# Twenty-five norms' rows transposed by DMA in two-byte halves instead of on TensorE

## The chip, the core and the metric

The kernel runs on one core of a Trainium2 chip, in one launch. The core has a matrix engine (TensorE, in the profile PE, with its weight loads as PEld), VectorE (DVE), ScalarE (ACT), GpSimd (POOL) and SyncE (SP), which here only issues DMAs. Each engine runs its own instructions in program order; they wait for one another by semaphores. Matmul results land in PSUM, everything else lies in SBUF. The metric is the device time of one execution in microseconds, the median of several runs.

## The reference

Eight batches of 512 rows with 256 features, fp32, go through four steps, each a normalisation of the rows and a residual addition:

```python
x = x + attn_a(layernorm(x), W_q, W_k, W_v)      # linear attention: q, k to unit length,
                                                 # q * sum over rows of (k * v) / 512
x = x + ffn(layernorm(x), W_r, W_k, W_v, mu_r, mu_k)
x = x + attn_b(layernorm(x), q_w, q_b, k_w, k_b, v_w, v_b, l_w, l_b)  # 16 heads of 64
x = x + ffn(layernorm(x), W_r, W_k, W_v, mu_r, mu_k)

def ffn(x):                                      # x_prev: the row before, zero for the first
    xr = mu_r * x + (1 - mu_r) * x_prev
    xk = mu_k * x + (1 - mu_k) * x_prev
    return sigmoid(xr @ W_r.T) * (relu(xk @ W_k.T) ** 2 @ W_v.T)

def attn_b(x):                                   # softmax over the queries (axis 2)
    scores = (x q_w + q_b) (x k_w + k_b).T / 8
    return concat(softmax(scores, axis=2) @ (x v_w + v_b)) @ l_w.T + l_b
```

There are therefore 4 x 8 = 32 layernorms. After each one a matmul over the features follows, so the normalised rows are needed with the features on the partitions: they have to be transposed.

## The kernel before, in words

Work goes in halves of a batch: h is 0 or 1, a half has 256 rows, two tiles of 128 rows by 256 features. The names a, f, n and g stand for the norms before the linear attention, the first feed-forward part, the softmax attention and the second feed-forward part; a tile's name ends in batch or half number.

`normed_t` (from L348) makes one half of a norm: VectorE takes mean and variance (L354, L355), GpSimd raises the variance to the power -0.5 (L373 to L375), ScalarE writes the normalised rows `xn` (L378), and TensorE turns them in four 128x128 transposes into one PSUM bank `tr_...` (L386). What reads that bank depends on the norm. For a (`linear`, L513) and n (`front`, L593) ScalarE copies it into SBUF (L519 into `xp`, L612 into `xta`). In `ffn` (L414, for f and g) ScalarE scales it twice straight from PSUM (L429), VectorE mixes PSUM and the scaled, shifted rows into `xk` and `xr` (L443), and only then is the bank given back.

The softmax attention runs in pairs of heads. `scores` (L907) multiplies keys and queries into a PSUM pair (L919), VectorE takes the maxima (L924), `exps` (L929) lets ScalarE exponentiate and sum (L935), GpSimd divides v by the sums (`scale_v`, L952), and `context` (L959) multiplies (L972). `attend` (L985) writes these in a fixed order for two pairs of heads.

All other work is put between these stretches by a planner that runs while the program is built. Every chain of steps (`linear`, `queries`, `front`, `ffn`, `project_pairs`, `values_fast`, `project_out`) is a Python generator that yields, before each step, the engine (T, A, V, G), the step's cost in microseconds and the time its input is ready. `Order` keeps a clock for each engine and picks the step to write next, with due dates in periods (one period for each two pairs of heads). `fill` writes whatever is ready beside the current TensorE time, `until` what is due, `CHOICES` holds for each period three numbers that vary its share of work, its slack and the order of equals. Since every engine runs in the order written, the order is fixed before the kernel starts. The costs decide the order; the waits at run time are semaphores.

[...] three pairs of banks that scores take turns on, and two single ones for the contexts; products and transposes borrow free ones. SBUF buffers `xn`, `xp`, `xr`, `xk` exist in two sets, "False" and "True"; `r` shares memory with `xk`, and `ka` with `xn`. The set "True" serves batch 1's front and, later, the g norms of batches 0 to 6.

SyncE issues the weights and inputs at the start, later each half's output (L876) and, when both halves of a batch are out, the load of the batch four further on (L264).

Of the kernel before, what the change touches and what calls it, by code (L numbers as in the profile page):

```python
# [7 lines left out]

F32 = mybir.dt.float32
AF = mybir.ActivationFunctionType  # L10
ALU = mybir.AluOpType
AX = mybir.AxisListType

P = 128
B, S, D = 8, 512, 256
# [13 lines left out]
CHANGE = 0.1  # L29
PAIRS, BANKS = 3, 2  # L30
X_LANDS = (4.1, 8.5, 12.0)
PASS = {"T": 0.27, "A": 0.2, "V": 0.17, "G": 0.17}

CHOICES = (
    (-2, 1, 55171), (-6, 2, 40869), (0, 0, 0), (-2, 1, 0), (0, -1, 58232), (6, 0, 85741),
    (6, -1, 2853), (0, 0, 0), (-6, -1, 27454), (0, -1, 74092), (0, 0, 2161), (2, 1, 0), (6, 0, 0),
    (-6, 0, 93887), (0, 0, 0), (4, 2, 61401), (0, 0, 0), (1, 1, 45112), (-2, 0, 99964),  # L40
    (-1, 0, 87739), (0, 0, 37516), (6, -1, 75545), (2, -1, 48345), (-1, 0, 55064), (0, -1, 12544),
    (-4, 0, 88217), (0, 0, 0), (4, 2, 76141), (1, 0, 10517), (4, -1, 38996), (6, 1, 66702),
    (-4, 0, 67700), (0, 0, 0), (0, 0, 0),
)


# [27 lines left out]
class Order:  # L74
# [3 lines left out]


    def __init__(self):  # L80
        self.free = {"T": 0.0, "A": 0.0, "V": 0.0, "G": 0.0}
        self.chains, self.period, self.spent, self.count = [], -1, 0.0, 0
        self.marks = {None: 0.0}

        self.banks = [0.0] * (PAIRS + BANKS)
        self.current, self.at = None, 0.0
# [103 lines left out]
    def fill(self, budget=0.0, slack=1.0):  # L190


        begin = self.spent
        late = {"V": slack, "A": slack, "G": slack + 2.0}
        while True:
            a = [
                c for c in self.able(2 * (budget - (self.spent - begin)))
                if (self.start(c) <= self.now + 0.2 if c.on == "T"
                    else self.start(c) + c.cost <= self.now + late[c.on])
            ]  # L200
            if not a:
                return
            self.run(self.first(a))
# [24 lines left out]
def kernel(ctx: ExitStack, tc: tile.TileContext, a: dict, out: bass.AP):  # L228
# [116 lines left out]

        return t[:, h, :].rearrange("p (t d) -> p t d", t=2)

    def normed_t(src, name, s, h, ready, mark=None, early=False):  # L348

        ready = yield "V", 1.2, ready  # L350
        mv = small.tile([P, 2, 2], F32, tag="mv", name=f"mv_{name}_{h}")
        for u in range(2):
            st = small.tile([P, 6], F32, tag="st", name=f"st_{name}_{h}_{u}")
            nc.vector.bn_stats(st, src[:, 2 * h + u, :])  # L354
            nc.vector.bn_aggr(mv[:, u, :], st)  # L355
        xn, rstd = inner(s["xn"], h), small.tile([P, 2], F32, tag="rstd", name=f"rstd_{name}_{h}")
        if early:

            ready = yield "G", 1.05, ready
            nc.gpsimd.tensor_scalar(rstd, mv[:, :, 1], LN_EPS, 1.0, ALU.add, ALU.mult)  # L360
            nc.gpsimd.tensor_tensor(rstd, rstd, neg_half[:, :2], ALU.pow)
            ready = yield "V", 0.75, ready
            for u in range(2):
                nc.vector.tensor_scalar(
                    xn[:, u, :], src[:, 2 * h + u, :], mv[:, u, 0:1], rstd[:, u : u + 1],
                    ALU.subtract, ALU.mult,
                )
        else:

            shift = small.tile([P, 2], F32, tag="shift", name=f"shift_{name}_{h}")  # L370
            nc.vector.tensor_scalar(shift, mv[:, :, 0], -1.0, None, ALU.mult)
            ready = yield "G", 1.3, ready
            nc.gpsimd.tensor_scalar(rstd, mv[:, :, 1], LN_EPS, 1.0, ALU.add, ALU.mult)  # L373
            nc.gpsimd.tensor_tensor(rstd, rstd, neg_half[:, :2], ALU.pow)
            nc.gpsimd.tensor_tensor(shift, shift, rstd, ALU.mult)  # L375
            ready = yield "A", 1.0, ready
            for u in range(2):
                nc.scalar.activation(  # L378
                    xn[:, u, :], src[:, 2 * h + u, :], AF.Identity,
                    bias=shift[:, u : u + 1], scale=rstd[:, u : u + 1],  # L380
                )
        ready = yield "T", 0.55, ready, -1, mark
        ps = bank(f"tr_{name}_{h}").rearrange("p (k s) -> p k s", k=KC)
        for kc in range(KC):
            for u in range(2):
                nc.tensor.transpose(  # L386
                    ps[:, kc, u * P : (u + 1) * P], xn[:, u, kc * P : (kc + 1) * P], ident
                )
        return ps, ready

    def rows(name, lhs, rhs):

# [18 lines left out]

    edge = {}

    def ffn(xb, name, s, h, ready, add_on):  # L414


        ps, ready = yield from normed_t(xb, name, s, h, ready)

        parts = ((1, s["xn"]), (0, s["xp"]))
        if not edge:  # L420
# [19 lines left out]
        for (i, y), dst in zip(parts, (xk, xr)):  # L440
# [5 lines left out]
                )  # L446
            if i == 1:
                mixed = ready
        order.give()
        done = yield "T", BANK, mixed  # L450
        ps = bank(f"k_{name}_{h}")
        for dc in range(KC):
# [49 lines left out]
    def adder(b):  # L502

        return nc.vector if b < 2 else nc.gpsimd
# [8 lines left out]
    def linear(b, h):  # L513

        xb, s = x[b], buffers(b == 1)
        ps, ready = yield from normed_t(xb, f"a{b}", s, h, asked[b] + X_LANDS[min(b, 2)] + h / 2, early=b < 2)
        xt, kv = inner(s["xp"], h), inner(s["ka"], h)
        ready = yield "A", 0.5, ready
        nc.scalar.copy(xt, ps)  # L519
        order.give()  # L520
        order.marks[f"a{b}", h] = ready
        ss = small.tile([P, 2], F32, tag="ss", name=f"ssk_{b}_{h}")
        arrived = ready
        for u in range(2):
            ready = yield "T", BANK, arrived
            ps = bank(f"kv_{b}_{h}_{u}")
            for kc in range(KC):
                nc.tensor.matmul(  # L528
                    ps, lhsT=xt[:, kc, u * P : (u + 1) * P], rhs=wkv[:, kc, :],
                    start=(kc == 0), stop=(kc == KC - 1),  # L530
                )
            ready = yield "A", 0.8, ready
            vs = two.tile([P, D], F32, tag="av", name=f"av_{b}_{h}_{u}")
            nc.scalar.copy(vs, ps[:, D:])
            sq = one.tile([P, D], F32, tag="sq", name=f"sqk_{b}_{h}_{u}")
            nc.scalar.activation(sq, ps[:, :D], AF.Square, accum_out=ss[:, u : u + 1])
            if u == 1:
                order.add(queries(b, h), *due_of(b))
            ready = yield "V", 0.35, ready
            nc.vector.tensor_mul(kv[:, u, :], ps[:, :D], vs)  # L540
            order.give()
        rn = small.tile([P, 2], F32, tag="rn", name=f"rnk_{b}_{h}")
        ready = yield from power(rn, ss, b, h, 0, ready)

        for u in range(2):
            ready = yield "V", 0.39, ready
            if b not in means:
                means[b] = kv[:, u, :]
                nc.vector.tensor_scalar(means[b], kv[:, u, :], rn[:, u : u + 1], None, ALU.mult)
            else:  # L550
                nc.vector.scalar_tensor_tensor(
                    means[b], kv[:, u, :], rn[:, u : u + 1], means[b], ALU.mult, ALU.add
                )
        if both(f"a{b}"):
            order.add(mean(b, ready), *due_of(b))
# [37 lines left out]
    def front(b, h, gf, ready):  # L593
# [7 lines left out]
                qs[:, u, :], qs[:, u, :], rn[:, u : u + 1], gf, ALU.mult, ALU.mult  # L601
            )
        ready = yield from add_to(xb, h, s["r"][:, h, :], ready, adder(b))
        ready = yield from ffn(xb, f"f{b}", s, h, ready, adder(b))


        last = f"qk_{NP * (b - 1) - 2}" if b > 1 else None
        ps, ready = yield from normed_t(xb, f"n{b}", s, h, ready, last)
        ready = yield "A", 0.5, ready
        if b not in xta:  # L610
            xta[b] = two.tile([P, KC, S], F32, tag="xta", name=f"xta_{b}")
        nc.scalar.copy(xta[b][:, :, h * HS : (h + 1) * HS], ps)  # L612
        order.give()
        order.marks[f"n{b}", h] = ready
        if not both(f"f{b}"):
            if b == 0:
# [251 lines left out]
    def tail(b, h, ready):  # L868

        last = b == B - 1  # L870

        add_on = nc.vector if last else nc.gpsimd
        yield from ffn(x[b], f"g{b}", buffers(not last), h, ready, add_on)
        ts = slice(2 * h, 2 * h + 2)
        rows_out = out[b].rearrange("(t p) d -> p t d", p=P)
        nc.sync.dma_start(out=rows_out[:, ts, :], in_=x[b][:, ts, :])  # L876
        if both(f"g{b}") and b + 4 < B:
            load_x(b + 4)
            add_front(b + 4)
# [105 lines left out]
    def attend(g):  # L985

        for c in range(NT):
# [5 lines left out]
            else:  # L993
                order.fill(BANK)
            exps(g, c)
            order.fill()
        for c in range(NT):
            scores(g + 1, c)
            if c == 1:
# [3 lines left out]
            if c == 3:  # L1003
                context(g, 3)
            exps(g + 1, c)
            order.fill()


    G = B * NP
# [23 lines left out]


    total = B * (2.2 + 6 * BANK + 42 * FAST + 0.43 + 8 * BANK + 2 * FFN) - 4 * BANK - 2 * FFN
    total += 2 * FAST
    for first in range(0, G, 2):
        g = order.period = first + 1
# [73 lines left out]
```

## Time and profile before

| What | us |
|---|---|
| median of three runs (1163.23 to 1165.66) | 1163.61 |
| the profiled execution, its own time | 1162.87 |
| its span, first to last instruction | 1161.0 |
| ScalarE: exps L935, 512 instructions | 346.6 busy |
| VectorE: maxima L924, 256 instructions | 309.2 busy |
| TensorE: scores L919, contexts L972 | 262.9 and 260.3 busy |
| TensorE: transposes L386, the four groups of 56 for a, f, n and g | 9.5, 8.5, 8.3 and 8.2 busy, 273 to 299 ns each |
| GpSimd: scaling of v L952, 128 instructions | 78.7 busy |

The profile is of one execution, so sums are made against its own time. The granted TensorE clock was 0.999 of full speed. A duration in the tables is that of one instruction; matmuls overlap one another in the pipeline, so their durations add up to more than the time that they take, and the distance between the starts of neighbours says what one of them costs. "Idle before" a group is time in which its engine stood still just before the group's instructions, with the instruction that ended the wait. An engine's idle time costs nothing as long as TensorE has work.

### The profile page before, as it was taken

To read this page: it belongs to the slowest core of one execution; us is meant where nothing else is said; L and a number is where in the kernel's file an instruction comes from. 1 tells how busy PE (TensorE), PEld (TensorE's weight loads), DVE (VectorE), ACT (ScalarE), POOL (GpSimd) and SP (SyncE) were. 2 spreads that over 40 slices of the span, in tenths; PEclk is the share of its full clock that TensorE was granted. 3 is DMA by queue.
4 is the path that set the end of the run, shared out by engine and by line. 5 is a ranking of instruction groups with operands and counts; after the bars stand their busy time and mean duration, and the time that the engine had idled before them with its cause. 6 is when DMAs were issued, how large, how long until landed. Compare 5 with 4: busy or idle time off the path is not lost.

```text
span 1161.0 us, 19258 instructions
## 1 busy us (share of the span) xinstructions
PE 1143.5 (98%) x7212; PEld 719.5 (62%) x7212; DVE 772.9 (67%) x1384; ACT 679.3 (59%) x1776; POOL 422.7 (36%) x602
## 2 busy tenths in 40 slices
PE   6999999999999999999999999999999999999998
PEld 3655466655667566666666666766557666666657
DVE  5677675766667677575777674757757666657754
ACT  4557664766545756456655574755764565654743
POOL 5374243523335233443333433323344223332311
PEclk9999999999999999999999999999999999999999
DMA  8000000000000000000000000000000000000001
GB/s 294 1 1 2 1 1 1 2 1 10 28 1 1 2 1 10 28 1 1 2 10 1 28 1 1 10 2 28 1 1 19 1 1 1 1 10 10 1 1 37
DMA packets 10491, 16.04 MB, mean 14 GB/s; under 512 B 768, under 2 KB 8960, under 8 KB 9888
## 3 DMA queue, kind: packets, MB, share of 16 engines
q1 hardware_dynamic: 9248, 13.11, 3.3%
q8 instruction: 57, 0.93, 0.3%
q10 hardware_dynamic: 864, 1.05, 0.3%
q0 software_dynamic: 288, 0.67, 0.2%
q14 instruction: 34, 0.28, 0.1%
HBM read 10.63 MB, written 4.19 MB: 13 GB/s over the span
## 4 chain that ended last, share of the span: by engine, by line
PE 94%; DVE 4%; issue 0%; ACT 0%; POOL 0%; DMA 0%; DVEq 0%; POOLq 0%; ACTq 0%
PE sc L919 20%; PE cx L972 19%; PE m_qk L763 15%; PE y L397 10%; PE m_v L798 7%; PE kv L528 5%; PE q L397 2%; PE r_g L397 2%; PE r_f L397 2%; PE k_g L454 2%; PE o_f L397 2%; PE k_f L454 2%; PE o_g L397 2%; PE tr_f L386 1%; PE qk L891 1%; PE tr_a L386 1%
## 5 line engine op out<-in xcount | busy, mean ns | idle before, releaser
L935 ACT ACTIVATE e<-sc,nm 128x512 f32<-128x512 f32 x512 | 346.6, 689 | 127.4 <-DVE nm L924 125.4
L924 DVE TENSOR_REDUCE nm<-sc 128x2 f32<-128x1024 f32 x256 | 309.2, 1218 | 81.6 <-PE sc L919 80.7
L919 PE MATMUL sc<-qk 64*64 64x512 f32 x2048 | 262.9, 594 | 0.8 <-DVE qk L740 0.8
L972 PE MATMUL cx<-e,vs 64*64 64x512 f32 x2048 | 260.3, 590 | 0.0
L952 POOL TENSOR_TENSOR vs<-v,rs 128x256 f32<-128x256 f32 x128 | 78.7, 616 | 438.5 <-DVE rs L948 413.9
L972 PEld LDWEIGHTS cx<-e,vs 64*64 64x64 f32 x2048 | 81.4, 133 | 138.5 <-issue 120.1
L919 PEld LDWEIGHTS sc<-qk 64*64 64x64 f32 x2048 | 72.6, 132 | 138.0 <-issue 87.8
L397 PE MATMUL y<-al,ctx 128*128 128x256 f32 x512 | 116.2, 380 | 0.0
L397 PEld LDWEIGHTS y<-al,ctx 128*128 128x128 f32 x512 | 96.9, 190 | 15.7 <-ACT e L935 1.6
L935 ACT ACTIVATION_READ_ACCUMULATOR e<-sc,nm 128x1 f32 x512 | 105.1, 205 | 0.0
L980 DVE TENSOR_TENSOR ctx<-cx,ctx 128x512 f32<-128x512 f32 x64 | 44.3, 692 | 46.8 <-ACT ctx L979 46.8
L731 POOL TENSOR_TENSOR qk<-qk,qk 128x512 f32<-128x512 f32 x31 | 39.5, 1274 | 63.5 <-ACT qk L728 60.3
L861 DVE TENSOR_TENSOR x<-y,x 128x512 f32<-128x512 f32 x32 | 22.1, 690 | 49.5 <-PE y L397 49.3
L528 PE MATMUL kv<-wkv,xpFalse 128*128 128x512 f32 x112 | 52.9, 603 | 0.1
L979 ACT COPY ctx<-cx 128x512 f32<-128x512 f32 x64 | 37.3, 583 | 12.7 <-PE cx L972 12.7
L736 DVE TENSOR_TENSOR qk<-m_qk,qk 128x512 f32<-128x512 f32 x31 | 21.4, 691 | 32.0 <-PE m_qk L763 14.2
L733 POOL TENSOR_TENSOR qk<-qk 128x512 f32<-128x512 f32 x31 | 39.4, 1270 | 2.4
L480 POOL TENSOR_TENSOR x<-x,xkFalse 128x512 f32<-128x512 f32 x24 | 31.1, 1295 | 21.3 <-DVE xkFalse L473 11.5
L763 PE MATMUL m_qk<-xta,aq 128*128 128x256 f32 x124 | 38.7, 393 | 0.0
L728 ACT COPY qk<-m_qk 128x512 f32<-128x512 f32 x31 | 18.3, 590 | 34.3 <-PE m_qk L763 34.2
L763 PE MATMUL m_qk<-xta,sums_q 128*128 128x256 f32 x124 | 37.1, 381 | 1.0 <-DVE qk L722 0.6
L763 PE MATMUL m_qk<-xts,aq 128*128 128x256 f32 x124 | 37.2, 382 | 0.2
(238 smaller groups left out, 1960.5 us busy)
## 6 DMA issues: line engine op xcount, KB each, us to landing
out<-x SPq DMA_DIRECT2D x16, 256.0 KB, 2.1
x<-in_x SPq DMA_DIRECT2D x6, 512.0 KB, 4.4
aq<-in_aq SPq DMA_DIRECT2D x1, 1024.0 KB, 8.1
ak<-in_ak SPq DMA_DIRECT2D x1, 1024.0 KB, 10.1
av<-in_av SPq DMA_DIRECT2D x1, 1024.0 KB, 12.2
al<-in_al SPq DMA_DIRECT2D x1, 1024.0 KB, 15.3
x<-in_x ACTq DMA_DIRECT2D x4, 128.0 KB, 4.0
x<-in_x SPq DMA_DIRECT2D x4, 128.0 KB, 3.9
```

Of the source, the lines that this page charges most:

```text
L397: nc.tensor.matmul(ps[:, u * D : (u + 1) * D], lhsT=lhs[i][:, u * P : (u + 1) * P], rhs=rhs[i], start=(i == 0), stop=(i == n - 1),)
L454: nc.tensor.matmul(ps[:, dc * HS : (dc + 1) * HS], lhsT=fk[:, kc, dc * P : (dc + 1) * P], rhs=xk[:, kc, :], start=(kc == 0), stop=(kc == K ...
L528: nc.tensor.matmul(ps, lhsT=xt[:, kc, u * P : (u + 1) * P], rhs=wkv[:, kc, :], start=(kc == 0), stop=(kc == KC - 1),)
L731: nc.gpsimd.tensor_tensor(c12, c12, c22, ALU.add)
L763: nc.tensor.matmul(ps[:, w * HS : (w + 1) * HS], lhsT=lhs[w][n - 1], rhs=block_of_rows(b, n), start=True, stop=True,)
L798: nc.tensor.matmul(ps[:, u * HS : (u + 1) * HS], lhsT=block_of_rows(b, n)[:, u * P : (u + 1) * P], rhs=rhs[n - 1], start=True, stop=True,)
L919: nc.tensor.matmul(ps[m * HD : (m + 1) * HD, j, :], lhsT=kt[hs, keys], rhs=qt[hs, :], start=True, stop=True,)
L924: nc.vector.tensor_reduce(nm, ps, AX.X, ALU.max, negate=True)
L935: nc.scalar.activation(e[:, j, :], ps[:, j, :], AF.Exp, bias=nm[:, j : j + 1], accum_out=sums[g, h][:, c % 2, j : j + 1],)
L952: nc.gpsimd.tensor_tensor(vs, vh[b, p // 4][:, 2 * h : 2 * h + 2, cols].rearrange("p t (j d) -> p t j d", j=2), rs.unsqueeze(3).to_broadca ...
L972: nc.tensor.matmul(cx[m][j * HD : (j + 1) * HD, :], lhsT=vsc[g, c // 2][ks, c % 2, j, :], rhs=es[g, c][ks, j, :], start=(c == 0), stop=(c ...
L980: nc.vector.tensor_tensor(ct, cx[1], ct, ALU.add)
```

## The change

For the norms a, f and n of batches 2 to 7 and g of batches 0 to 6, that is 6 x 3 + 7 = 25 norms or 50 halves, the rows are no longer turned by TensorE. `normed_t` is cut in two: `normed` makes the rows, `normed_t` turns them as before, and the new `normed_dma` turns them in this way:

- GpSimd takes the fp32 rows as two-byte words and writes all low words of a block beside one another, then all high words, into `xr` (two copies of 512 words a partition).
- SyncE issues a DMA transpose of the 128 x 1024 words from `xr` into `xk`: eight blocks of 128x128.
- ScalarE joins the two words of each number again in one copy of 1024 words: for f and g into `xr`, for a into `xp`, for n into `xta`.

In `ffn` the later steps then read `xr` in SBUF where they read the PSUM bank; for a and n the joining copy replaces the copy out of PSUM. The a, f and n norms of batches 0 and 1 and the g norm of batch 7 stay on TensorE.

The planner gets a fifth engine S for SyncE, on which a transpose costs 0.9 us and its result is reckoned ready 2.0 us later. The numbers in `CHOICES` are new, and inside `attend` the calls of `fill` get a slack of 2.8 instead of 1.0 for steps beside scores; the planner's sum of TensorE's work falls by 6 x 3.3 + 7 x 1.1 us.

```diff
-PASS = {"T": 0.27, "A": 0.2, "V": 0.17, "G": 0.17}
+PASS = {"T": 0.27, "A": 0.2, "V": 0.17, "G": 0.17, "S": 2.0}
...
-        late = {"V": slack, "A": slack, "G": slack + 2.0}
+        late = {"V": slack, "A": slack, "G": slack + 2.0, "S": slack + 2.0}
...
+    def normed_dma(src, name, s, h, ready, dst, mark=None):
+
+
+        ready = yield from normed(src, name, s, h, ready)
+        apart, turned = (s[n].bitcast(U16)[:, h, :] for n in ("xr", "xk"))
+        ready = yield "G", 1.8, ready
+        for u in range(2):
+            nc.gpsimd.tensor_copy(
+                apart.rearrange("p (l k u d) -> p l k u d", l=2, k=KC, u=2)[:, :, :, u, :],
+                s["xn"].bitcast(U16)[:, h, u, 2:].rearrange("p (k d l) -> p l k d", l=2, k=KC),
+            )
+        ready = yield "S", 0.9, ready
+        nc.sync.dma_start_transpose(
+            out=turned.rearrange("p (g r) -> p g r", r=P), in_=apart
+        )
+        ready = yield "A", 0.9, ready, -1, mark
+        nc.scalar.copy(
+            dst().rearrange("p k (s l) -> p l k s", l=2),
+            turned.rearrange("p (l k s) -> p l k s", l=2, k=KC),
+        )
+        return ready
...
-    def ffn(xb, name, s, h, ready, add_on):
+    def ffn(xb, name, s, h, ready, add_on, by_dma):
...
-        ps, ready = yield from normed_t(xb, name, s, h, ready)
+        if by_dma:
+            ps = chunks(s["xr"], h)
+            ready = yield from normed_dma(
+                xb, name, s, h, ready,
+                lambda: s["xr"].bitcast(U16)[:, h, :].rearrange("p (k s) -> p k s", k=KC),
+            )
+        else:
+            ps, ready = yield from normed_t(xb, name, s, h, ready)
...
-        order.give()
+        if not by_dma:
+            order.give()
...
-        ps, ready = yield from normed_t(xb, f"a{b}", s, h, asked[b] + X_LANDS[min(b, 2)] + h / 2, early=b < 2)
+        ready = asked[b] + X_LANDS[min(b, 2)] + h / 2
...
+        if b < 2:
+            ps, ready = yield from normed_t(xb, f"a{b}", s, h, ready, early=True)
+            ready = yield "A", 0.5, ready
+            nc.scalar.copy(xt, ps)
+            order.give()
+        else:
+            ready = yield from normed_dma(
+                xb, f"a{b}", s, h, ready, lambda: s["xp"].bitcast(U16)[:, h, :, 2:]
+            )
...
-        ready = yield from ffn(xb, f"f{b}", s, h, ready, adder(b))
+        ready = yield from ffn(xb, f"f{b}", s, h, ready, adder(b), b >= 2)
...
+        if b < 2:
+            ps, ready = yield from normed_t(xb, f"n{b}", s, h, ready, last)
+            ready = yield "A", 0.5, ready
+            nc.scalar.copy(of_half()[:, :, h * HS : (h + 1) * HS], ps)
+            order.give()
+        else:
+            ready = yield from normed_dma(
+                xb, f"n{b}", s, h, ready,
+                lambda: of_half().bitcast(U16)[:, :, h * S : (h + 1) * S], last,
+            )
...
-        yield from ffn(x[b], f"g{b}", buffers(not last), h, ready, add_on)
+        yield from ffn(x[b], f"g{b}", buffers(not last), h, ready, add_on, not last)
...
-            order.fill()
+            order.fill(0.0, 2.8)
...
+    total -= 6 * 3.3 + 7 * 1.1
```

## Prediction

> **What bounds the kernel now.** I read the page's busy times first, then the chain of work that ended last, then the groups by shape, then who waits for whom, then SyncE's own waits.
>
> ```profile
> PE 1143.5 (98%) x7212; PEld 719.5 (62%) x7212; DVE 772.9 (67%) x1384; ACT 679.3 (59%) x1776; POOL 422.7 (36%) x602
> ...
> PE 94%; DVE 4%; issue 0%; ACT 0%; POOL 0%; DMA 0%; DVEq 0%; POOLq 0%; ACTq 0%
> ```
>
> TensorE has work in 1143.5 of 1161.0 us, and 94% of the chain is its own matmuls. Of the 17.5 us idle, 6.3 stand before the first transpose. So time leaves this kernel almost only by taking work off TensorE, and returns as soon as a wait reaches it.
>
> What a transpose costs is not its duration (273 ns) but its place in TensorE's queue, because matmuls are pipelined. The chain (start, length, what) shows that place:
>
> ```profile
> 32.08 1.73 PE k_f L454 x8
> 33.80 0.44 PE tr_f L386 x4
> 34.24 1.72 PE kv L528 x4
> ...
> 94.17 1.73 PE m_qk L763 x8
> 95.90 0.44 PE tr_a L386 x4
> ```
>
> Four transposes, one half of a norm, push the next matmul back by 0.44 us, between neighbours that run without a gap.
>
> The groups by shape (line, engine, operation, count, busy us, mean ns, idle before) price the new work:
>
> ```profile
> L612 ACT COPY xta<-tr_n 128x512 f32<-128x512 f32 x16 | 9.3, 587 | 19.4 <-PE tr_n L386 19.4
> L1024 ACT ACTIVATE aq<-aq 128x1024 f32<-128x1024 f32 x2 | 2.0, 1064 | 0.0
> L421 POOL TENSOR_SCALAR fv<-fv 128x512 f32<-128x512 f32 x1 | 1.5, 1529 | 0.1
> L443 DVE SCALAR_TENSOR_TENSOR xkFalse<-tr_f,mu,xnFalse 128x256 f32<-128x256 f32 x28 | 12.2, 479 | 8.4 <-ACT xpFalse L429 8.2
> L551 DVE SCALAR_TENSOR_TENSOR xnFalse<-xnFalse,rnk 128x256 f32<-128x256 f32 x21 | 11.6, 553 | 0.5
> ```
>
> Then the waits (who, for whom: us in total, times, longest), the first three of the engines, the next two of SyncE's queue, and last one DMA row of the page (engine, operation, count, KB, us to landing):
>
> ```profile
> PEld sc L919 <- ACT e L935: 42.7, 95, 0.8
> PEld m_qk L763 <- ACT e L935: 13.0, 16, 0.8
> POOL vs L952 <- DVE rs L948: 413.9, 94, 12.5
> ```
> ```profile
> SPq L876 <- POOL x L480: 867.0, 13, 136.8
> SPq L264 <- DMA out<-x: 6.9, 4, 1.8
> ```
> ```profile
> out<-x SPq DMA_DIRECT2D x16, 256.0 KB, 2.1
> ```
>
> The two weight-load rows say that ScalarE's exps are on time by only a little: they hold a weight load back 111 times, never above 0.8 us, and mostly under running matmuls. GpSimd waits 413.9 us before its scaling of v alone, so it has room. SyncE does nothing but outputs and reloads.
>
> [...] L551, both inputs in SBUF, averages 553 ns, against 479 for L443, whose first input is PSUM.
>
> **The change, part by part.** It moves 50 halves: a, f and n of six batches are 36, g of seven is 14. The order view confirms 200 fewer matmuls on TensorE, 100 more copies on GpSimd, 50 DMA transposes on SyncE, 26 more instructions on ScalarE.
>
> *Transposes removed.* 50 x 0.436 us (0.109 us between starts of neighbours in the trace, four a half) = 21.8 us, all on the path that sets the end. Each also held a PSUM bank until it was read; that freedom I count at nothing.
>
> *GpSimd split.* Two copies a half of 128x512 two-byte elements, no row of the same kind. [...] From above: L421, one input of 512 fp32 elements, 1.53 us. I take 0.9, the planner's value in the diff[...]. 100 x 0.9 = 90 us[...], so GpSimd goes from 423 to about 513 us, 45% of the span: no bound. Behind a pair of copies (1.8 us) the scaled v can queue, for which context matmuls wait: the likely collision.
>
> *DMA transposes.* 256 KB each on SyncE. From below: the plain 256 KB store, 2.1 us from issue to landing. [...] I take 3.0[...]; the planner reckons with 0.9 + 2.0 = 2.9. A transfer beside running matmuls costs nothing as long as it lands when the planner expects it. If not, its joining copy stands at the head of ScalarE's queue, with exps, the relu and tanh of other halves and the qk copies behind it, and TensorE waits for those: lateness times 50, times the share that ScalarE's gaps don't absorb. No row gives that share; I take a third (bounds 0 and 1).
>
> *SyncE's queue.* The transposes now stand behind outputs and reloads. A reload waits for the output's landing, 1.8 us at worst, four times: 7 us at most, one half each, mostly absorbed. The 867 us of output waits don't simply carry over: the planner now places transposes at the point where their data are ready, and an output only after its addition has been issued.
>
> *ScalarE join.* L1024 gives 1.06 us for 1024 elements from SBUF[...]. In f and g 26 copies are new: 27.7 us. In a and n 24 replace a 0.59 us copy: 24 x 0.47 = 11.4 us. Total 39 us, ScalarE from 679 to about 718 of 1140 us, 63%. Strided two-byte writes may cost more; an end of 2.1 us a copy (twice the row) would add 53 us, 68% busy, still not a bound. The cover is the room between the score stretches. In the order view, between the first and last exp of each pair of heads, stand 71 other ScalarE instructions instead of 66 (63 of them ctx copies in both), so the wider allowance puts only five more there.
>
> *VectorE and ScalarE mixing.* In f and g 104 mixes now have two SBUF inputs: 553 - 479 = 74 ns each, 8 us. ScalarE's 104 scalings read SBUF instead of PSUM: between 0 and 12 us (0.48 us now, 0.60 in the SBUF normalisation L378). Neither engine binds; hidden behind matmuls. If that cover goes, each delays one k product by about 0.1 to 0.3 us.
>
> *Searched order.* A new list shifts products and chain steps. I see no sum in it: the same work fills TensorE. From below -5 us (regained idle), from above +10, middle +1.
>
> *Longer chains.* A half now takes 1.8 + 3.0 + 0.5 = 5.3 us longer in a and n (half a microsecond for the slower copy), less about 0.5 for the transpose; in f and g 1.8 + 3.0 + 1.06 - 0.5 = 5.4. The trace's chains have room: in the timeline batch 5's transposes of a stand at 507 and 537 us, those of n at 608 and 652, under a period of some 140 us a batch. The first two batches and the last tail, where idle is real, are left as they are.
>
> Sum, from this profiled execution: span 1161.0 - 21.8 + 1 (order) + 2 (scaled v and late joins, about a quarter more on top of the 8.7 us of weight loads that wait for it) = 1142.2. Around the span lie 1162.87 - 1161.0 = 1.9 us, giving 1144.1. The median of the three runs, 1163.61, is 0.7 above the profiled run, so 1145.
>
> **Rivals.** R1, slower: *the late join*. One mechanism: the DMA transpose lands after the planner's 2.9 us, and ScalarE stands at the joining copy. At 5.5 us it is 2.6 late; 50 x 2.6 / 3 = 43 us; with the gain of 19, 1163.6 + 24 = 1188. It decides from 50 x d / 3 = 19, d = 1.1 us, a landing of 4.0 us. For it: [...]exps with under a microsecond to spare. Against it: [...]ScalarE's 41% idle.
>
> R2, much slower: the eight blocks go in turn[...].
>
> R3, about no change: *GpSimd late*. Copies at 1.53 us make 3.1 us a half, 13% of the span in 50 blocks; 128 scalings of v x 13% x half a block (1.5 us) = 25 us if none is absorbed, 1145 + 20 = 1165. Against it: 413.9 us of waiting before those scalings.
>
> That the rows are not moved at all is excluded by the order view.
>
> **How the numbers follow.** Forecast 0.68; R3 0.09 (a third on each side and within); R1 0.15; R2 0.08. Within 0.2% (2.3 us) is what a measurement of this kernel can't tell from no change. Faster 0.68 + 0.03 = 0.71, same 0.03 and 0.01 from R1's edge = 0.04, slower 0.25. The likeliest case's own range is 1138 (5 us of idle regained, no late joins) to 1153. For 8 in 10 it must take in R3 and most of R1: 1138 to 1195.
>
> **What would show it.** Right: TensorE 200 matmuls fewer and about 22 us shorter; transposes landing in 2.5 to 3.5 us; joining copies near 1.06 us; ScalarE's idle before them under 0.5 us each; GpSimd near 510 us. Wrong: a wait of joins on the DMA above 50 us in all, weight loads waiting for exps well above 56 us, or for vs well above 9.

## The result and the profile after

The changed kernel takes 1161.14 us (median of 20 runs, 1158.35 to 1164.38) against 1165.28 us (20 runs, 1163.01 to 1166.10) for the kernel before on the same chips: ratio 0.9973, 95% interval 0.9965 to 0.9981. It is faster, by 4 us. The forecast was 1145, some 19 us faster. The sign was right and the size was not: most of the expected gain went somewhere. The executions of the changed kernel fall into groups by their granted clock: seven at 0.994 took 1162.5 to 1164.4 us, twelve at 0.996 or 0.997 took 1160.3 to 1162.2, and one at 0.999 took 1158.4.

The two executions that were profiled, 1162.87 us before and 1162.71 changed, lie only 0.2 us apart. The tables below therefore have to explain a gain that is missing altogether; by the medians, 4 us of it arrived.

The page of the changed kernel, busy times and chain:

```profile
PE 1129.8 (97%) x7012; PEld 703.9 (61%) x7012; DVE 806.4 (69%) x1384; ACT 730.6 (63%) x1802; POOL 485.7 (42%) x702
...
PE 46%; DVE 2%; issue 1%; ACT 1%; DVEq 0%
```

The chain's shares add up to 50% only, because it could be followed back no further than to a mix at 574 us; they can't be set beside the 94% of before. The 200 matmuls are gone, and TensorE's share of the span has not risen. VectorE, which was to gain 8 us of work, has 33.5 more. The groups by shape show where. The mixes, L443 before, are L479 now (line, engine, operation, count, busy us, mean ns, idle before):

```profile
L479 DVE SCALAR_TENSOR_TENSOR xrTrue<-xrTrue,mu,xpTrue 128x256 f32<-128x256 f32 x28 | 24.5, 916 | 0.0
L479 DVE SCALAR_TENSOR_TENSOR xrFalse<-xrFalse,mu,xpFalse 128x256 f32<-128x256 f32 x24 | 21.0, 916 | 0.0
L479 DVE SCALAR_TENSOR_TENSOR xkTrue<-xrTrue,mu,xnTrue 128x256 f32<-128x256 f32 x28 | 19.2, 727 | 0.3
L479 DVE SCALAR_TENSOR_TENSOR xkFalse<-xrFalse,mu,xnFalse 128x256 f32<-128x256 f32 x24 | 15.6, 691 | 0.3
L479 DVE SCALAR_TENSOR_TENSOR xkTrue<-tr_f,mu,xnTrue 128x256 f32<-128x256 f32 x4 | 1.7, 476 | 1.3 <-ACT xpTrue L465 1.3
```

The first four rows are the 104 mixes of DMA halves, both inputs in SBUF; the last is a mix whose half still comes from PSUM. Same shape, same operation, 476 ns there and 691 to 916 here. Mean times count gives 84.6 us for the 104, against 49.5 at 476 ns: 35 us more. (The busy column counts time in which two records overlap only once.) The spread view (duration in ns: min/median/max, first and last start) says what kind of slowness it is:

```profile
L479 DVE SCALAR_TENSOR_TENSOR xkTrue<-xrTrue,mu,xnTrue x28: 473/484/1541, 287.8 to 1083.8; 128x256 f32<-128x256 f32 x28
L479 DVE SCALAR_TENSOR_TENSOR xrFalse<-xrFalse,mu,xpFalse x24: 471/546/1510, 163.7 to 931.7; 128x256 f32<-128x256 f32 x24
```

Not every mix is slow. The fastest takes what it took from PSUM, the slowest three times that. I counted over the starts and ends of the records: 45 of the 104 begin while no GpSimd instruction runs, and average 0.478 us; 59 begin beside one, and average 1.069. Of the 59, 13 begin beside a GpSimd instruction on two elements a partition (L374 to L376 and L547), and none of these takes longer than 0.484; the other 46 average 1.235. The timeline around 779 us shows such a pair (start, length, engine, line, what):

```profile
777.07 1.89 DVE L479 SCALAR_TENSOR_TENSOR xkFalse<-xrFalse,mu,xnFalse 128x256 f32<-128x256 f32 x2
777.20 1.48 POOL L783 TENSOR_TENSOR v<-v 128x512 f32<-128x512 f32 x1 [3.79 <-ACT v L780]
...
778.75 1.33 POOL L785 TENSOR_TENSOR v<-v 128x512 f32<-128x512 f32 x1
778.88 2.90 DVE L479 SCALAR_TENSOR_TENSOR xrFalse<-xrFalse,mu,xpFalse 128x256 f32<-128x256 f32 x2
...
780.05 1.45 POOL L783 TENSOR_TENSOR qk<-qk,qk 128x512 f32<-128x512 f32 x1
781.57 1.33 POOL L785 TENSOR_TENSOR qk<-qk 128x512 f32<-128x512 f32 x1
```

Two mixes that need just under 1.0 us together take 2.90. The single records show when they are let go: the GpSimd multiplications end at 778.68, 780.09 and 781.49 us, and the three long mixes end at 778.96, 780.37 and 781.78, each 0.28 to 0.29 us later. So do 43 of the 59, whatever they have waited. This holding back of a mix until a GpSimd instruction has ended is called the lock below. The partner is mostly old work. In 31 of the 59 cases it is L783 or L785, two multiplications that the kernel before had too; the new two-byte copies (L405) are the partner twice in this order, though in e10's order below (there L406) they are it 18 times in 54.

What TensorE waited for directly, in the changed kernel, before, and in the first experiment below, where the mixes are free (who, for whom: us in total, times, longest):

```profile
PE sc L971 <- DVE qk L792: 8.3, 5, 3.4
...
PE m_qk L815 <- DVE v L788: 3.9, 2, 2.0
```
```profile
PE sc L919 <- DVE qk L740: 0.8, 1, 0.8
```
```profile
PE sc L976 <- DVE qk L797: 4.1, 2, 3.4
```

Before, scores waited 0.8 us for the same addition; now 8.3. The additions L788 and L792 follow other work in VectorE's fixed queue, and around 575, 780 and 1079 us that work includes mixes that GpSimd held up. Half of the 8.3 us is something else: the third row shows that 4.1 us stay when the mixes are free, among them the longest wait, 3.4 us at 131 us. VectorE and GpSimd just before it, in the changed kernel:

```profile
130.54 0.95 DVE L372 TENSOR_SCALAR shift_f<-mv_f 128x2 f32<-128x2 f32 x1
131.41 1.88 DVE L643 SCALAR_TENSOR_TENSOR xkFalse<-xkFalse,rnq,gf 128x256 f32<-128x256 f32 x2
131.55 1.46 POOL L785 TENSOR_TENSOR qk<-qk 128x512 f32<-128x512 f32 x1
```

L643 is old work with two SBUF inputs (L600 before). Its second instruction took 1.48 us and also ended 0.28 us after the multiplication beside it; L372, 0.17 us at the median, took 0.95 beside the one before. So here the new order made an old pair of instructions meet GpSimd.

A balance over TensorE puts this together. I added, for every matmul, the usual distance to the next start between neighbours of its shape without a gap (0.109 us for a transpose), and took the rest of the distances as lost:

| us | before | changed |
|---|---|---|
| first matmul starts | 6.3 | 6.4 |
| work at the usual distances | 1120.4 | 1098.6 |
| lost between matmuls | 29.3 | 49.3 |
| after the last start | 5.0 | 6.5 |
| span | 1161.0 | 1160.8 |

The transposes are counted here at the forecast's own distance, so the 21.8 us of the second row are its sum again and no check of it. What is new is the third row: 20.0 us came back as distances between matmuls. About 5 of them are no waits but matmuls that ran at half the clock for 10.2 us (last section).

### The profile page after: what moved, and what is told of

Same layout as the page of the kernel before. It is cut to its first block, busy times and chain, and to the rows that moved or that the text cites. A ratio compares the mean times of both kernels' runs of the same rounds, so it can differ in the third digit from the quotient of the medians.

```text
span 1160.8 us, 19186 instructions
## 1 busy us (share of the span) xinstructions
PE 1129.8 (97%) x7012; PEld 703.9 (61%) x7012; DVE 806.4 (69%) x1384; ACT 730.6 (63%) x1802; POOL 485.7 (42%) x702
## 4 chain that ended last, share of the span: by engine, by line
PE 46%; DVE 2%; issue 1%; ACT 1%; DVEq 0%
PE cx L1024 10%; PE sc L971 10%; PE m_qk L815 8%; PE y L426 5%; PE m_v L850 4%; PE r_g L426 2%; PE o_g L426 2%; PE k_g L491 1%; PE r_f L426 1%; PE kv L571 1%; PE o_f L426 1%; PE k_f L491 1%; PE q L426 1%; DVE xrFalse L479 1%; DVE xrTrue L479 0%
## 5 line engine op out<-in xcount | busy, mean ns | idle before, releaser
L971 PE MATMUL sc<-qk 64*64 64x512 f32 x2048 | 270.5, 600 | 9.4 <-DVE qk L792 8.3
L1024 PE MATMUL cx<-e,vs 64*64 64x512 f32 x2048 | 268.2, 594 | 0.2 <-POOL vs L1004 0.2
L1024 PEld LDWEIGHTS cx<-e,vs 64*64 64x64 f32 x2048 | 85.4, 134 | 139.9 <-issue 115.9
L426 PE MATMUL y<-al,ctx 128*128 128x256 f32 x512 | 116.3, 380 | 0.0
L426 PEld LDWEIGHTS y<-al,ctx 128*128 128x128 f32 x512 | 96.8, 190 | 17.3 <-ACT e L987 3.2
L783 POOL TENSOR_TENSOR qk<-qk,qk 128x512 f32<-128x512 f32 x31 | 40.8, 1315 | 27.8 <-ACT qk L780 26.2
L405 POOL COPY xrFalse<-xnFalse 128x512 uint16<-128x512 uint16 x72 | 42.6, 626 | 8.1 <-ACT xnFalse L379 8.1
L785 POOL TENSOR_TENSOR qk<-qk 128x512 f32<-128x512 f32 x31 | 40.6, 1310 | 2.4
L815 PE MATMUL m_qk<-xts,aq 128*128 128x256 f32 x124 | 37.1, 381 | 3.9 <-DVE v L788 3.9
L815 PE MATMUL m_qk<-xta,aq 128*128 128x256 f32 x124 | 38.2, 390 | 0.0
L815 PE MATMUL m_qk<-xta,sums_q 128*128 128x256 f32 x124 | 36.9, 379 | 0.0
```

The costliest lines, as they stand in the source:

```text
L405: nc.gpsimd.tensor_copy(apart.rearrange("p (l k u d) -> p l k u d", l=2, k=KC, u=2)[:, :, :, u, :], s["xn"].bitcast(U16)[:, h, u, 2:].rear ...
L426: nc.tensor.matmul(ps[:, u * D : (u + 1) * D], lhsT=lhs[i][:, u * P : (u + 1) * P], rhs=rhs[i], start=(i == 0), stop=(i == n - 1),)
L783: nc.gpsimd.tensor_tensor(c12, c12, c22, ALU.add)
L815: nc.tensor.matmul(ps[:, w * HS : (w + 1) * HS], lhsT=lhs[w][n - 1], rhs=block_of_rows(b, n), start=True, stop=True,)
L971: nc.tensor.matmul(ps[m * HD : (m + 1) * HD, j, :], lhsT=kt[hs, keys], rhs=qt[hs, :], start=True, stop=True,)
L1024: nc.tensor.matmul(cx[m][j * HD : (j + 1) * HD, :], lhsT=vsc[g, c // 2][ks, c % 2, j, :], rhs=es[g, c][ks, j, :], start=(c == 0), stop=(c ...
```

## The experiments

Ten runs. The first four were made to choose between the mixes (A), late joins on ScalarE (B), and a new order that waits for GpSimd's queue (C).

**e1: the mix with one input.** The order of the changed kernel; the mix of a DMA half becomes an operation of VectorE on `y` alone, the term with mu left out.

```diff
             for kc in range(KC):
+                if by_dma:
+                    nc.vector.tensor_reduce(
+                        dst[:, kc, :], y[:, h, kc, :HS].unsqueeze(2), AX.X, ALU.add
+                    )
+                    continue
```

> The changed kernel in its own order, but in the 104 mixes of the moved f and g halves VectorE only copies the scaled, shifted rows (a reduction over one element, one SBUF input) instead of adding mu times the joined rows; the mu term is left out. Theory A, VectorE and GpSimd exclude each other (the mix now has two SBUF inputs): the mix falls from 0.81 us to below 0.5 us, no copy of it above 0.6 us, and the time falls by 8 to 16 us against the changed kernel, to about 0.985 to 0.990 of the kernel before. Theory B, late joins on ScalarE: the mix may get shorter but the time stays at 0.997. Theory C, the new order itself waits for the queue of GpSimd at the ends of periods: stays at 0.995 to 0.998.

Measured: 1148.13 us, ratio 0.9855 (0.9840 to 0.9869). Its spread view:

```profile
L480 DVE TENSOR_REDUCE xkTrue<-xnTrue x28: 402/410/421, 287.6 to 1070.8; 128x256 f32<-128x256 f32 x28
L480 DVE TENSOR_REDUCE xrTrue<-xpTrue x28: 404/408/412, 288.3 to 1071.4; 128x256 f32<-128x256 f32 x28
```

Every instruction takes 0.41 us, whatever GpSimd does, and 13 us of the kernel's time come back, as A expected; B and C expected no change. The gaps between matmuls fall from 49.3 to 36.3. One thing is not clean: the substitute is also 0.07 us shorter than an undisturbed mix, 7 us over the 104.

**e2: a short join.** The join copies only the 512 high words and leaves out the low ones.

```diff
         nc.scalar.copy(
-            dst().rearrange("p k (s l) -> p l k s", l=2),
-            turned.rearrange("p (l k s) -> p l k s", l=2, k=KC),
+            dst().bitcast(F32),
+            turned.bitcast(mybir.dt.bfloat16).rearrange("p (l k s) -> p l k s", l=2, k=KC)[:, 1],
         )
```

> The changed kernel in its own order, but the joining copy takes only the high two-byte words (512 elements instead of 1024, read as bf16), so the low halves of the numbers are left out; it should take about 0.65 us instead of 1.34. Theory A (VectorE and GpSimd exclude each other): at most 3 us faster than the changed kernel, 0.995 to 0.998 of the kernel before. Theory B (late joins on ScalarE, each 0.44 us longer than planned): the 50 copies give back 35 us of ScalarE time and the time falls by 8 to 15 us, to 0.985 to 0.990. Theory C: no change, 0.997.

Measured: 1160.06 us, ratio 0.9961 (0.9947 to 0.9974), so 1 us less than the changed kernel. One of its four groups of joins:

```profile
L414 ACT CAST xrTrue<-xkTrue 128x512 f32<-128x512 bf16 x14 | 8.6, 616 | 10.2 <-DMA xkTrue<-xrTrue 10.2
```

The joins took 0.62 us instead of 1.34, 36 us less ScalarE in all, and almost nothing reached the end. B falls as far as it means the length of a join; the joins' waits for their DMA are the same as in the changed kernel, some 42 us.

**e3 and e4: the lock without the DMA.** The kernel before, its order and its transposes. In both ScalarE copies the f and g halves from PSUM into `xr` as well; in e3 the mix reads that copy, in e4 it still reads PSUM.

```diff
+        moved = name[0] == "f" and int(name[1:]) >= 2 or name[0] == "g" and name != f"g{B - 1}"
+        if moved:
+            nc.scalar.copy(chunks(s["xr"], h), ps)
...
-                    dst[:, kc, :], ps[:, kc, :], mu[:, i, kc : kc + 1], y[:, h, kc, :HS],
+                    dst[:, kc, :], chunks(s["xr"], h)[:, kc, :] if moved else ps[:, kc, :],
+                    mu[:, i, kc : kc + 1], y[:, h, kc, :HS],
```

> The kernel before in its own order, all transposes on TensorE, but in the f norms of batches 2 to 7 and the g norms of batches 0 to 6 ScalarE also copies the transposed rows from PSUM into SBUF (0.6 us, 26 times) and VectorE mixes from that copy. Theory A: the mixes rise from 0.476 to 0.7 us or more and the time rises by 5 to 15 us over the kernel before (1.005 to 1.013), clearly more than the control without the SBUF mix. Theories B and C: rises by no more than the control, 1.000 to 1.004.

> Control to the one before: the kernel before with the same 26 extra copies on ScalarE into SBUF, but VectorE mixes from PSUM as it did. Theory A: mixes stay at 0.476 us, time within 3 us of the kernel before (0.999 to 1.003). Theory B: ScalarE's lateness reaches TensorE and most of 26 x 0.6 = 16 us shows, 1.006 to 1.013.

Measured: e3 1173.28 us, ratio 1.0079 (1.0067 to 1.0091); e4 1166.93, ratio 1.0017 (1.0008 to 1.0026). The same group in e3 and then in e4:

```profile
L446 DVE SCALAR_TENSOR_TENSOR xrTrue<-xrTrue,mu,xpTrue 128x256 f32<-128x256 f32 x28 | 19.5, 738 | 0.0
```
```profile
L446 DVE SCALAR_TENSOR_TENSOR xrTrue<-tr_g,mu,xpTrue 128x256 f32<-128x256 f32 x28 | 12.1, 474 | 0.0
```

Moving one input of a mix from PSUM to SBUF costs 6.3 us by itself, or 8 where the two are compared at the same granted clock (1173.0 to 1173.3 against 1164.9 to 1165.6 us, all at 1.000), with no DMA transpose, no two-byte copy and no new order anywhere in the kernel.

**e5: only a and n by DMA**, so that no mix reads two SBUF inputs. The order is searched anew (other `CHOICES`), with the durations that the trace showed as the planner's costs.

```diff
-        ready = yield from ffn(xb, f"f{b}", s, h, ready, adder(b), b >= 2)
+        ready = yield from ffn(xb, f"f{b}", s, h, ready, adder(b), False)
...
-        yield from ffn(x[b], f"g{b}", buffers(not last), h, ready, add_on, not last)
+        yield from ffn(x[b], f"g{b}", buffers(not last), h, ready, add_on, False)
...
-    total -= 6 * 3.3 + 7 * 1.1
+    total -= 6 * 2.2
```

> Only the 24 halves of a and n go by DMA; f and g keep their TensorE transposes, so every mix reads PSUM as before. The order is searched anew, with the durations measured in the changed kernel (join 1.35, split 1.3, issue 1.23 us). If VectorE's and GpSimd's exclusion is what took the gain: 24 x 0.436 = 10.5 us off 1165, so 1152 to 1157, and mixes at 0.48 us. If the DMA transposes, splits or joins themselves cost the time: half of the changed kernel's loss stays, 1159 to 1164.

Measured: 1158.34 us, ratio 0.9940 (0.9923 to 0.9956), between the two cases: 1.3 us above what the exclusion alone would give, 0.7 below what a cost of the DMA path would. Mixes are back at 0.474 to 0.480 us. Its gaps are 35.2 us against 29.3 before, so some 6 us are lost to the new order or to the DMA path. This run doesn't say to which; e9 and e10 at least separate the order from the place of the operand.

**e6 and e7: the scaled rows in PSUM.** All 50 halves go by DMA and the whole computation is done. In f and g of DMA halves ScalarE writes the scaled, shifted rows `y` into a borrowed PSUM bank, so that a mix has one input in each memory. Column 0, the row before the half, is set by VectorE, and the planner lets ScalarE's step wait for a free bank. e6 and e7 are two orders from one search, with the measured durations as costs.

```diff
+        for i, dst in ((1, xk), (0, xr)) if by_dma else ():
+            ready = yield "A", 1.2, ready, -1, None, True
...
+            y = bank(f"y{i}_{name}_{h}").rearrange("p (k s) -> p k s", k=KC)
+            for kc in range(KC):
+                nc.scalar.activation(
+                    y[:, kc, 1:], ps[:, kc, : HS - 1], AF.Identity, scale=omu[:, i, kc : kc + 1]
+                )
+            ready = yield "V", 1.1, ready, -1, (name, 0)
...
+                nc.vector.scalar_tensor_tensor(
+                    dst[:, kc, :], ps[:, kc, :], mu[:, i, kc : kc + 1], y[:, kc, :],
+                    ALU.mult, ALU.add,
+                )
+            order.give()
```

> All 50 halves by DMA, but in f and g ScalarE writes the scaled half of the mix into a PSUM bank, so a mix has one SBUF and one PSUM input; the computation is whole. The order is searched anew with measured durations. If the exclusion is what took the gain: as with one input, 1145 to 1152, mixes at 0.48 us whatever GpSimd does. If the second SBUF input is not the point, but mixing from a DMA'd tile or the fuller ScalarE: mixes near 0.8 us and 1156 to 1164.

> The same kernel with another order from the same search, to see what an order alone makes. If orders of about equal planned length differ by little on the chip: within 3 us of the first. If the order is as large a cause as the exclusion: 8 us or more apart.

Measured: 1154.86 and 1155.27 us, ratios 0.9906 (0.9891 to 0.9921) and 0.9912 (0.9894 to 0.9929). Mixes at 0.478 us as the exclusion asks, but the time of e6 is 3 us above what I expected and lies between its two cases. The two orders lie 0.4 us apart, within the 3 expected of e7; but both have the same long wait near 164 us, so they say little of what another order can do. The windows of e6 show one loss (from:to, length, busy time of PE, PEld, DVE, ACT and POOL, granted clock, DMA share, GB/s):

```profile
150.00:161.00 11.00, 11.00 (x53) 9.68 (x52) 8.57 (x21) 4.05 (x10) 7.95 (x14) 1.00 0.00 0
165.00:168.00 3.00, 2.85 (x16) 1.03 (x20) 0.89 (x2) 0.00 (x0) 1.71 (x3) 0.50 0.00 0
168.00:171.00 3.00, 3.00 (x16) 0.75 (x14) 0.81 (x2) 1.45 (x4) 0.00 (x0) 0.50 0.00 0
```

TensorE waited 3.3 us at 162 us for L823, the addition that is L792 in the changed kernel, and then ran 6.8 us at half its clock. The lock has no part in this wait: VectorE itself had stood idle for 3.6 us until the GpSimd multiplication L816 was done, and that took its usual 1.26 us.

**e8: the lock stays, the order knows its price.** The changed kernel's operations, with an order searched for mixes of 1.7 us a pair and for the measured join, split and issue.

```diff
-            ready = yield "V", 0.79, ready
+            ready = yield "V", 1.7 if by_dma else 0.79, ready
```

> The changed kernel's operations unchanged, two SBUF inputs in every mix of a DMA half, but the order is searched with 1.7 us for a pair of mixes instead of 0.79 (and join 1.35, split 1.3, issue 1.23). If what costs is that mixes come later than the order allows for: mixes still near 0.8 us each, but 1147 to 1154. If VectorE's added busy time costs by itself, or the search finds no room for it: 1157 to 1164.

Measured: 1157.19 us, ratio 0.9935 (0.9919 to 0.9951). The mixes still average 716 to 833 ns by group. The time lies at the lower edge of the second case, so neither case holds as I put it: against the changed kernel the order made with these costs saves 4 us of the 13, not all and not none. How much of the 4 is due to the mixes' price alone is not shown, since the other costs and the whole list of choices changed with it.

**e9 and e10: one order, two places.** e9 is e6 with an order searched for no long single wait of TensorE, and for 1.3 us instead of 0.79 for the pair L643. e10 has e9's order and instructions; `y` lies in SBUF.

```diff
-            y = bank(f"y{i}_{name}_{h}").rearrange("p (k s) -> p k s", k=KC)
+            order.take()
+            y = s["xn" if i else "xp"][:, h, :, :HS]
```

> As e6 (all 50 halves by DMA, the scaled half of the mix in PSUM), with an order searched so that no single wait of TensorE is long, and with 1.3 us instead of 0.79 for the query pair L643 that also reads two SBUF inputs. In e6 one wait of 3.3 us was followed by 6 us at half the granted clock. If that one place was what e6 lost: 1146 to 1151. If the losses of the new orders are spread: 1153 to 1157 as in e6.

> e9's instructions in e9's order; only the place of the scaled half differs: SBUF instead of PSUM, so that the 104 mixes have two SBUF inputs again. If the exclusion costs the time: 6 us or more above e9, mixes near 0.8 us. If the order was the cause and the second SBUF input is not: within 2 us of e9.

Measured: e9 1148.06 us, ratio 0.9866 (0.9851 to 0.9880); e10 1153.83, ratio 0.9911 (0.9895 to 0.9928). The spread views of one group in e9 and then in e10:

```profile
L484 DVE SCALAR_TENSOR_TENSOR xkTrue<-xrTrue,mu,y_g x28: 472/478/482, 222.7 to 1069.8; 128x256 f32<-128x256 f32 x28
```
```profile
L485 DVE SCALAR_TENSOR_TENSOR xkTrue<-xrTrue,mu,xnTrue x28: 472/706/1519, 226.4 to 1075.8; 128x256 f32<-128x256 f32 x28
```

In e9 54 mixes begin beside a running GpSimd instruction and average 0.478 us, as do the 50 others; in e10 the numbers are again 54 and 50, with 1.065 and 0.482. The order in which each engine runs its instructions is the same in both traces, record by record. So GpSimd beside a mix costs nothing by itself, and neither does a second SBUF input; the two together do. All 47 mixes of e10 that were lengthened end 0.27 to 0.29 us after the GpSimd instruction beside them. The place of one operand makes 5.8 us (I had said 6 or more), with 32 us more of mixing on VectorE. e9 computes the whole reference and is, with e1, the fastest: 15.7 us under the kernel before. It also falls in the first of its two cases; its gaps are 35.4 us against e6's 42.8, and e6's long wait and the half clock behind it come to 6.7. But the whole list of choices differs, so that this one place was the cause is not shown.

## Why the prediction was wrong in size

**The step that failed** is the one on "VectorE and ScalarE mixing", which said "553 - 479 = 74 ns each, 8 us" and "Neither engine binds; hidden behind matmuls". The term measured 35 us (0.81 us a mix on average, up to 1.54), and it was not hidden: e1 gave 13 us back, of the 16 by which the forecast missed. The fallback, "each delays one k product by about 0.1 to 0.3 us", had the wrong victim as well as the wrong size. In the changed kernel TensorE's new waits were for the additions L788 and L792 on VectorE, not for the mixes' own products.

Behind the difference between the prediction's two means, 553 ns for L551 with two SBUF inputs and 479 for L443 with one from PSUM, lies the lock: beside a running GpSimd instruction a mix averages 0.478 us in e9, where one input lies in PSUM, and 1.065 in e10, where both lie in SBUF. Only beside GpSimd's instructions on two elements a partition was no mix of the changed kernel lengthened, though by their records these last 0.2 to 0.8 us. What was wrong was the price: I took it from the mean of L551, a group that meets GpSimd less often (8 of its 21 instructions begin beside one, 59 of the 104 mixes). A blocked mix ends 0.28 us after the GpSimd instruction beside it, most often one of 1.3 to 1.5 us, so the price depends on how often they meet at the new place. The kernel before showed that its durations come in two kinds, had I asked for the spread instead of the mean:

```profile
L600 DVE SCALAR_TENSOR_TENSOR xkFalse<-xkFalse,rnq,gf x28: 455/480/1504, 22.3 to 879.8; 128x256 f32<-128x256 f32 x28
```
```profile
L443 DVE SCALAR_TENSOR_TENSOR xrTrue<-tr_g,mu,xpTrue x28: 468/476/477, 229.2 to 1085.8; 128x256 f32<-128x256 f32 x28
```

L600, two SBUF inputs, has a median of 480 ns and a longest of 1504; L443, one from PSUM, never leaves 468 to 477 in this group. A price of "between 74 ns and 1.0 us a mix, by how many meet" would have put up to 104 us on VectorE as the upper end.

**The other steps:**

- Transposes removed: 21.8 us forecast. The 200 matmuls are gone; their 21.8 us were not measured apart. TensorE's busy time fell by 13.7 us, not by the 22 named as a sign of being right; about 5 of the rest are the stretches at half clock.
- DMA transposes: 3.0 us forecast, an estimate; the trace before has no transpose by DMA, only the plain store's 2.1 us below it. All DMA transposes of these runs move two-byte words; that fp32 rows have to be split for them was not shown. The page of the changed kernel has, for the larger group, 36 issues and the median from issue to landing in us:

```profile
xkFalse<-xrFalse SPq DMA_TRANSPOSE x36, 3.1
```

- 46 of all 50 landed within 4.0 us, the slowest after 6.2. Rivals R1 (landing above 4.0 us) and R2 (later still) are therefore out. TensorE's matmuls on 128x256 (L426, L491, L815, L850) started 0.216 us apart at the median with a transpose in flight (331 distances) and without one (1964). ScalarE did stand 41.8 us before joins for the DMA, 0.8 us a join where 0.5 was named as right, and near the 50 named as a warning. TensorE itself waited 1.1 us for joins; no run takes ScalarE's waits away, so their share in the end is not shown.
- SyncE's queue: the reloads waited 7.4 us in all, where 7 was named as the most.
- GpSimd split: 0.9 us a copy forecast, 0.613 at the median. GpSimd is busy 485.7 us, not 513, and weight loads waited 10.1 us for the scaled v against 8.7. R3, late GpSimd, didn't happen. That the result lies near R3's 1165 has another cause, and R3's own working gave 25 us but carried on with 20.
- ScalarE join: 1.06 us forecast, 1.34 measured (the 2.1 of the upper bound was not needed). ScalarE reached 730.6 us instead of 718; e2, with 36 us less, puts the effect on the end at about 1 us.
- Searched order: +1 forecast. Not measured by itself. In the changed kernel one wait of 3.4 us at 131 us remains in e1, where the mixes are not blocked; it and the slow clock behind it make some 5 of e1's 36.3 us of gaps. e6 and e9 differ in their orders alone and lie 6.8 us apart (4.7 when each is taken as a ratio to the kernel before on its own chips), so an order's share can be about as large as the mixes'.

With the mixes free of the lock, e1 and e9 took 1148.1 us, 3 above the forecast and inside the range of its likeliest case, 1138 to 1153. This doesn't prove the sum: e6 and e7, whose mixes are as free, took 1154.9 and 1155.3, outside that range, and e1's substitute is shorter than a mix.

## What to carry to other kernels

Moving an operand from PSUM to SBUF changes more than where it lies: a two-input VectorE instruction that has both inputs in SBUF can be held until the GpSimd instruction beside it has ended (0.48 us became up to 1.54 here), so look at which GpSimd work runs beside it, and keep one input in PSUM if a bank is free. Price such an instruction by minimum, median and maximum, never by a mean from another place. When an order is planned from fixed costs, a duration that doubles without being in the plan can reach the end although its engine is idle for much of the span, because short additions for TensorE are queued behind it; here between a fifth and a third of the added VectorE time reached the end (6.3 of 23 us in e3 against e4, 5.8 of 32 in e10 against e9, 13 of 42 in the changed kernel against e1).

## What the runs showed that was not expected

A wait of TensorE can cost more than itself. Two windows after the 3.4 us wait of the changed kernel, and one after its 2.5 us wait at 575 us (columns as above):

```profile
134.00:137.00 3.00, 2.46 (x12) 0.79 (x16) 0.90 (x2) 0.00 (x0) 1.53 (x3) 0.50 0.02 5
137.00:140.00 3.00, 3.00 (x20) 0.97 (x16) 2.00 (x6) 1.45 (x4) 0.89 (x2) 0.50 0.00 0
```
```profile
578.00:581.00 3.00, 2.96 (x16) 1.04 (x20) 2.62 (x3) 0.00 (x0) 2.65 (x4) 0.50 0.03 5
```

By the clock's own record matmuls ran at half the clock for 6.8 us and for 3.4 us: about 3.4 and 1.7 us on top of the waits. After the waits of 2.0 and 1.9 us at 780 and 1079 us the clock stayed at 1.00, and so it did after a wait of 2.4 us near the start of the kernel before. But a wait of 1.9 us near the start of e1 was followed by 3.4 us at half clock, and e7 has such a stretch at 480 us with no single wait above 1.5 us before it. So the length of a wait doesn't decide.

What goes with the clock in these traces is how the waits lie between fixed steps of time. In each of the twelve traces the clock changes only at whole multiples of 3.41 us from its last change; in the changed kernel it stayed for 122.88, 6.83, 436.91, 3.41 and 576.85 us, which are 36, 2, 128, 1 and 169 times that. I cut the traces into these steps, from 12 us after the start to the last matmuls, and took the share of each in which TensorE was busy. Eleven steps at full clock were followed by one at half clock, and TensorE was busy in 20 to 45% of each (20% before the change at 134 us, 41% before the one at 578). Of the nearly 4000 others at full clock one was as low, at 45%, and the next lowest had 46%. Out of half clock, three steps at 68 to 79% busy were followed by another at half clock, eleven at 86 to 100% by full clock. The waits of 2.0 and 1.9 us at 780 and 1079 us, after which the clock stayed, each lay in two steps, busy to 80 and 61% and to 81 and 65%. This is read from the traces and was not tried by a run that inserts such a wait; what lowers the clock is not shown. Busy time is partly modelled, so the limits are approximate.

e9, whose waits after its start stay below 1.2 us, has a granted clock of 0.999 against 0.994 in the changed kernel.
